# Attention and feed-forward in one kernel: the last third of a head group's scores as one stretch, five steps a group

## Chip, cores and metric

One core of one Trainium2 chip. The metric is the device time of one execution in microseconds (us). The kernel before took 3215.65 us in the median of three runs (3213.75 to 3222.26).

## What is computed

A transformer block over 16 batches of 512 rows and 512 columns: layernorm, attention with 32 heads of 16 columns (rotary positions, causal mask, softmax), a projection, layernorm and the residual, then a gated feed-forward of 512 to 1408 to 512, again with layernorms and a residual. Cut to what matters here:

```python
q, k, v = (split_heads(norm(x) @ W.T + b) for each of q, k, v)   # 32 heads of 16
scores  = einsum('bhqd,bhkd->bhqk', rope(q), rope(k)) / sqrt(16)
weights = softmax(where(causal, scores, -inf))
out     = einsum('bhqk,bhkd->bhqd', weights, v)
x = x + norm(out @ Wo.T + bo)
g, u = (norm(x) @ gate_w.T) * gate_s, (norm(x) @ up_w.T) * up_s
x = x + norm(((silu(g) * u) @ down_w.T) * down_s)
```

## The kernel before

**Groups.** Four heads are a group, eight groups a batch (`NG`), 128 groups in all. Each head lies in 32 partitions of its tiles, so its matmuls use 32 rows of TensorE, and four heads can be at work there side by side. Scores are made twice. "s" has queries in the partitions; VectorE masks it in place and takes each row's negated maximum (`maxima`, line 607; in the profile the rows `s<-s,mask` and `nm<-`). "st" has keys in the partitions, with the maximum already taken off by a third matmul (`mx`, `one`); ScalarE makes exp of it (`weights`, line 631, `pt<-st`), GpSimd masks the diagonal (`pt<-pt`). An "s" score needs two matmuls (high and low part of k: kh, kl), an "st" score three (kh, kl, mx).

**Thirds and steps.** The causal half of the 512 x 512 scores is cut into three thirds (lines 35 and 36): one block 512 wide; two blocks 128 and 384 wide; one block 256 wide. A group has `STEPS` = 6 steps, two for each third. Step i belongs to third i // 2 and pair i % 2 of the heads: `scores` (line 562) makes "st" for two heads of group n and "s" for the other two heads of a later group m, which is n + 1 in steps 0 and 1 and n + 2 from step 2 on. The lists of up to four heads are issued in rounds, one matmul of each head in turn; where the lists differ in length the last rounds have two matmuls. Such a run of score matmuls is called a stretch here.

**PSUM.** There are eight banks: one "st" tile of two banks (`ps_t`, line 87, a single buffer), two "s" tiles of one bank, one for the value products ("av"), three for dense work (`ps_d`). A stretch waits until the exp and the maxima of the one before it have left these tiles.

**Order.** Every instruction is issued through `InOrder` (line 39; its line 49 is the one that the profile names for all), which keeps the order of the program on each engine. `one_step` (line 792) fixes that order: first what was put off to this step (`later`), at step 0 the loads of q, kh and kl of group n + 2 (`load_group`), then the stretch of scores, at step 2 the transposition of the next group's maxima (`turn_maxima`, sent by DMA at step 3 and read at the next group's step 0), then a share of dense work, then at step 3 `values` of the first third and at step 0 those of the second and third of the group before.

**Dense work.** Everything else that TensorE does (q, k, v, projection, gate, up, down, transpositions) is written as a list with costs (`MM` = 1, `M1` = 0.27 for the cheaper format, `TR` = 0.15). `run_list` (line 696) deals it out to the steps in equal shares; `batches` (line 951) makes one list for a batch's 48 steps, and a first list for 56 steps, from two groups ahead of the first batch on. Loads and stores stand in the same lists and go to SyncE's one queue in that order. A group's output is stored at the step after `values`; `sums` and `sums_2` (lines 678 and 687) fetch the softmax sums from DRAM 2 and 3 steps after it.

Of the kernel before, what the change touches and what calls it, by code (L numbers as in the profile page):

```python
# [10 lines left out]
FP = mybir.dt.float32  # L11
FR = mybir.dt.float32r
AF = mybir.ActivationFunctionType
# [5 lines left out]
P = 128  # L19
T = 512  # L20
# [5 lines left out]
NC = C // P  # L26
NG = H // 4
WIDTH = H * W + 32 - W + 1
STEPS = 6
MM = 1.0  # L30
TR = 0.15
M1 = 0.27
# [2 lines left out]
S_SETS = [[(3, 0, 512)], [(0, 384, 128), (2, 0, 384)], [(1, 0, 256)]]  # L35
ST_SETS = [[(0, 0, 512)], [(3, 0, 128), (1, 128, 384)], [(2, 0, 256)]]
# [15 lines left out]


class Block:

# [503 lines left out]

    def scores(self, n, m, i):

        third, pair = divmod(i, 2)
        ps = pm = None
        todo = []
        if 0 <= n < self.B * NG:
            ps = self.ps_t.tile([P, 2, T], FP, tag="st", name="st")
            q, ks, mx = self.qs[n], self.ks[n], self.mxs[n]
            for j in range(2):  # L570
                h = 32 * (2 * pair + j)
                r, r2 = slice(h, h + 32), slice(h, h + 2)
                todo.append([])
                for kb, at, w in ST_SETS[third]:
                    out, x = ps[:, j, at : at + w], q[r, T - w : T]
                    todo[-1] += [
                        (out, ks[0][r, ts(kb, P)], x, True, False),
                        (out, ks[1][r, ts(kb, P)], x, False, False),
                        (out, self.one[r2, :], mx[r2, T - w : T], False, True),
                    ]  # L580
        if 0 <= m < self.B * NG:
            if n < 0 and i % 2:
                both = self.ps_t.tile([P, 2, T], FP, tag="st", name="st")
                pm = [both[:, j, :] for j in range(2)]
            else:
                pm = [self.ps_s.tile([P, T], FP, tag="s", name="s") for _ in range(2)]
            q, ks = self.qs[m], self.ks[m]
            for j in range(2):
                h = 32 * (2 * (1 - pair) + j)
                r = slice(h, h + 32)  # L590
                todo.append([])
                for qb, at, w in S_SETS[third]:
                    out, x = pm[j][:, at : at + w], q[r, ts(qb, P)]
                    todo[-1] += [(out, x, ks[0][r, 0:w], True, False), (out, x, ks[1][r, 0:w], False, True)]

        for k in range(max((len(t) for t in todo), default=0)):
            for t in todo:
                if k < len(t):
                    out, l, r, first, last = t[k]
                    self.pe.matmul(out, l, r, start=first, stop=last)  # L600
        if ps is not None:
            self.weights(n, third, pair, ps)
        if pm is not None:
            for j in range(2):
                self.maxima(m, third, 2 * (1 - pair) + j, pm[j])

    def maxima(self, m, third, j, s):
        if m not in self.nms:
# [19 lines left out]

        self.later(1, put)

    def weights(self, n, third, pair, ps):
        w = sum(w for _, _, w in ST_SETS[third])
        if third < 2 or pair == 0:
            pt = self.tile([P, 2, T], "pt", bufs=4)
            self.pts[n, third, pair] = pt
        if third == 2:
            if pair:
                pt = self.pts[n, 2, 1] = self.pts[n, 2, 0]
            pt = pt[:, pair, :].rearrange("p (j t) -> p j t", j=2)
        self.act.activation(pt[:, :, :w], ps[:, :, :w], AF.Exp, scale=0.25)  # L640
        if third == 1:
            d = pt[:, :, 0 : 2 * P]
            pat = [[0, 2], [0, 2], [1, P]]
        else:
            d = pt[:, :, 0:P]
            pat = [[0, 2], [1, P]]
        self.pool.affine_select(out=d, in_=d, compare_op=ALU.is_ge, fill=0.0, base=0, pattern=pat, channel_multiplier=-1)

    def values(self, n, third):
        b, g = divmod(n, NG)  # L650
        if third == 0:
            self.avs[n] = self.ps_av.tile([P, T], FP, tag="av", name="av")
        av = self.avs[n]
        for kb, at, w in ST_SETS[third]:
            for j in range(4):
                h = 4 * g + j
                pt = self.pts[n, third, j // 2]
                pt = pt[:, j // 2, T // 2 * (j % 2) :] if third == 2 else pt[:, j % 2, :]
                self.pe.matmul(
                    av[32 * j : 32 * j + 32, T - w : T],  # L660
                    self.v17[b % 2][:, kb, h * W : h * W + 32],
                    pt[:, at : at + w],
                    start=(kb == 0),
                    stop=(third == 2),
                )
        for pair in range(2):
            del self.pts[n, third, pair]
        if third == 2:
            del self.ks[n], self.qs[n], self.mxs[n]
            ot = self.tile([P, T], "ot", bufs=1)  # L670
            self.act.copy(ot, self.avs.pop(n))
            i = (b % 2) * NC + g // 2
            self.later(1, lambda: self.sp.dma_start(out=self.od[i][P * (g % 2) : P * (g % 2) + P, :], in_=ot))
            if g % 2:

                self.later(8 if b == self.B - 2 and g < NG - 1 else 2, self.sums, b, g // 2)

    def sums(self, b, c):
        i = (b % 2) * NC + c
# [13 lines left out]
        self.later(2, lambda: self.pool.tensor_tensor(self.ocs[b, c], self.ocs[b, c], rc, ALU.mult))  # L693


    def run_list(self, L, steps):

        L = self.laid(L)
        total = sum(c for c, _ in L)
        done, i = 0.0, 0  # L700
        for s in range(steps):
            goal = total * (s + 1) / steps
            while i < len(L) and (done + L[i][0] / 2 < goal or s == steps - 1):
                L[i][1]()
                done += L[i][0]
                i += 1
            yield
# [242 lines left out]

    def batches(self):
        B = self.B
        work = self.run_list(self.first_list(), 56)
        self.load_group(0)
        for n, i0 in ((-2, 2), (-1, 0)):
            for i in range(i0, STEPS):
                self.one_step(work, n, i)
        for b in range(B):
            if b:
                if b < B - 1:  # L960
                    L = self.dense(b)
                    L += self.gate_ups(b - 1, b + 2 if b + 2 < B else None, b + 2 == B)
                    if b < B - 2:
                        L += self.downs(b - 1, b + 2)
                else:
                    down = [self.downs(b - 2, None, tbs, True, True) for tbs in ((0, 1), (2, 3))]
                    L = down[0] + self.dense(b, down[1]) + self.gate_ups(b - 1, None, True)
                work = self.run_list(L, NG * STEPS)
            for g in range(NG):
                for i in range(STEPS):  # L970
                    self.one_step(work, b * NG + g, i)
        L = [(0, lambda half=half: self.load_w(B - 1, "o", half)) for half in range(2)]
        work = self.run_list(L + self.downs(B - 2, None, (0, 1), True, True), STEPS + 2)
        for i in range(STEPS + 2):
            self.one_step(work, B * NG + i // STEPS, i % STEPS)
        for _, f in self.laid(self.last_list()):
            f()
# [61 lines left out]
```

## Time and profile before

| what | value |
|---|---|
| median of the runs | 3215.65 us |
| the profiled execution | 3215.86 us, its span 3214.0 us |
| mean granted TensorE clock | 0.984 |
| exp of 2 x 512 columns (`pt<-st`) | 1.024 us, 512 times |
| exp of 2 x 256 columns | 0.596 us, 256 times |
| maximum over 512, 384, 256, 128 columns (`s<-s,mask`) | 0.714, 0.567, 0.447, 0.312 us |
| reading out a maximum (`nm<-`) | 0.141 us, 2048 times |
| mask on GpSimd, 256 columns | 0.450 us, 512 times |

How to read it: "st<-q,kh" is a matmul that writes tile st from tiles q and kh; "PE" is TensorE's matmuls, "PEld" its weight loads, "DVE" VectorE, "ACT" ScalarE, "POOL" GpSimd, "SPq" SyncE's DMA queue. Matmuls overlap, so one matmul's duration is longer than the distance to the next start. A dense matmul in full fp32 stands as two records.

In the steady part a step's stretch starts after these medians from the last one, steps 0 to 5: 5.03, 3.67, 3.83, 4.78, 3.29 and 3.28 us. From a stretch's first start to the next dense start it takes 0.89 us (512 wide), 1.06 us (128 and 384) and 0.55 us (256 wide, steps 4 and 5).

### The profile page before, as it was taken

The page shows a single profiled execution, that of the slowest core. Times are in us where ns is not written, and L with a number is a line of the kernel's source. Part 1 is how long each engine was busy: PE and PEld are TensorE (multiplying, and loading weights), DVE is VectorE, ACT ScalarE, POOL GpSimd, SP SyncE. Part 2 cuts the span into 40 slices and gives each one's busy share as a digit, 9 for nine tenths or more (in the row PEclk, how much of TensorE's full clock was granted, in tenths as well). Part 3 has the DMA queues.
Part 4 walks back from the last instruction along what each step waited for, and adds up shares of the span by engine and source line. Part 5 has one row for each costly group of instructions (what it writes and reads, how often), then busy time and mean ns, then how long its engine had stood idle before and what let it go on. Part 6 is the DMA issues. An engine that isn't in the chain of part 4 may idle for free.

```text
span 3214.0 us, 59287 instructions
## 1 busy us (share of the span) xinstructions
PE 3097.9 (96%) x21258; PEld 1743.3 (54%) x21258; DVE 1888.0 (59%) x5911; ACT 1542.7 (48%) x2243; POOL 1383.9 (43%) x1933
## 2 busy tenths in 40 slices
PE   6889999999999999999999999999999999999988
PEld 2334555646556464655646455464655646455556
DVE  5465656556565665656566565665656566565633
ACT  5354545454554544545454554544455454453432
POOL 4143445443544534345443544534345453443343
PEclk9899999999999999999999999999999999999999
DMA  6454534445353443525345352543535345343422
GB/s 251 166 166 152 189 101 163 139 149 172 108 190 106 160 164 123 195 93 177 127 152 173 127 185 96 168 147 123 195 101 183 122 147 172 123 156 105 131 97 71
DMA packets 227441, 471.41 MB, mean 147 GB/s; under 512 B 40976, under 2 KB 45072, under 8 KB 226704
## 3 DMA queue, kind: packets, MB, share of 16 engines
q1 hardware_dynamic: 226704, 466.47, 43.1%
q8 instruction: 170, 2.79, 0.4%
q10 hardware_dynamic: 432, 1.05, 0.1%
q14 instruction: 135, 1.11, 0.1%
HBM read 345.79 MB, written 125.30 MB: 147 GB/s over the span
## 4 chain that ended last, share of the span: by engine, by line
PE 83%; DVE 2%; DMA 2%; ACT 2%; POOL 1%; issue 1%; SPq 0%; ACTq 0%; DVEq 0%; POOLq 0%
PE st L49 16%; PE pu L49 11%; PE pg L49 10%; PE av L49 9%; PE pd L49 9%; PE po L49 7%; PE pq L49 6%; PE pv L49 5%; PE pk L49 5%; PE s L49 3%; DMA kl<-kd 2%; PE px L49 1%; ACT pt L49 1%; DVE s L49 1%; PE pm L49 1%
## 5 line engine op out<-in xcount | busy, mean ns | idle before, releaser
L49 DVE CUSTOM_DVE_ANT_0 s<-s,mask 128x512 f32<-128x512 f32 (+1 forms) x2034 | 974.9, 510 | 713.8 <-PE s L49 530.8
L49 ACT ACTIVATE pt<-st 128x1024 f32<-128x1024 f32 (+1 forms) x768 | 677.0, 882 | 755.9 <-PE st L49 746.9
L49 POOL TENSOR_SCALAR_AFFINE_SELECT pt<-pt 128x256 f32<-128x256 f32 (+1 forms) x768 | 393.8, 513 | 1202.3 <-ACT pt L49 1200.0
L49 PEld LDWEIGHTS st<-q,kh 32*128 32x128 f32 x2048 | 191.3, 183 | 463.3 <-issue 225.6
L49 PE MATMUL st<-q,kh 32*128 32x512 f32 (+3 forms) x2048 | 411.2, 398 | 22.3 <-ACT pt L49 20.9
L49 PE MATMUL s<-kh,q 32*128 32x512 f32 (+1 forms) x2034 | 411.6, 399 | 17.2 <-DVE nm L49 8.8
L49 PE MATMUL s<-kl,q 32*128 32x512 f32 (+1 forms) x2034 | 340.7, 321 | 11.2 <-DMA kl<-kd 11.2
L49 PE MATMUL av<-pt,v 128*32 128x512 f32 (+3 forms) x4096 | 336.0, 447 | 0.0
L49 PE MATMUL st<-q,kl 32*128 32x512 f32 (+3 forms) x2048 | 333.5, 322 | 0.0
L49 PE MATMUL st<-mx,one 2*128 2x512 f32 (+3 forms) x2048 | 333.0, 321 | 0.0
L49 POOL TENSOR_TENSOR hl<-ht,hh 128x512 fp32r<-128x512 f32 (+1 forms) x192 | 229.6, 1196 | 184.3 <-ACT hh L49 176.7
L49 PE MATMUL pd<-wd,hl 128*128 128x512 f32 x704 | 288.9, 410 | 9.2 <-POOL hl L49 9.2
L49 PE MATMUL pd<-wd,hh 128*128 128x512 f32 x704 | 290.9, 413 | 2.2 <-ACT hh L49 2.2
L49 DVE DVE_READ_ACCUMULATOR2_ANT nm<- 128x1 f32 x2048 | 288.8, 141 | 0.0
L49 PE MATMUL pg<-xntf,wf 128*128 128x512 f32 x704 | 287.4, 408 | 1.5 <-ACT xntf L49 1.5
L49 PE MATMUL pu<-xntfl,wf 128*128 128x512 f32 x704 | 284.3, 404 | 0.0
L49 PE MATMUL pu<-xntf,wf 128*128 128x512 f32 x704 | 283.9, 403 | 0.0
L49 PE MATMUL pg<-xntfl,wf 128*128 128x512 f32 x704 | 281.5, 400 | 0.6 <-DVE xntfl L49 0.6
L49 PE MATMUL po<-w,oc 128*128 128x512 f32 x512 | 244.6, 610 | 3.7 <-DMA w<-in_wo 3.7
L49 PE MATMUL pq<-xnta,w 128*128 128x512 f32 x480 | 237.6, 626 | 6.9 <-ACT xntf L49 6.3
L49 PE MATMUL pk<-xnta,w 128*128 128x512 f32 x480 | 238.3, 615 | 4.3 <-DVE ya L49 3.7
L49 POOL TENSOR_TENSOR yl<-ya,yh 128x512 fp32r<-128x512 f32 x128 | 163.3, 1276 | 169.4 <-ACT yh L49 169.4
(118 smaller groups left out, 5021.8 us busy)
## 6 DMA issues: line engine op xcount, KB each, us to landing
wf<-wgs SPq DMA_DIRECT2D x176, 512.0 KB
q<-qd SPq DMA_DIRECT2D x128, 256.0 KB
kh<-kd SPq DMA_DIRECT2D x128, 256.0 KB
kl<-kd SPq DMA_DIRECT2D x128, 256.0 KB
od<-ot SPq DMA_DIRECT2D x128, 256.0 KB
w<-in_wo SPq DMA_DIRECT2D x34, 512.0 KB
xr<-in_x SPq DMA_DIRECT2D x66, 256.0 KB
w<-in_wq SPq DMA_DIRECT2D x32, 512.0 KB
```

Of the source, the lines that this page charges most:

```text
L49: return self.tc.keep_in_program_order(f(*args, **kwargs))
```

## The change

The last third gets one step for all four heads: `STEPS` is 5. The four heads' lists are issued in rounds of four, each list first the three "st" matmuls of a head of group n, then the two "s" matmuls of the same head of group m. Both write the same bank: "s" its first 256 columns, "st" its last 256. Heads 0 and 1 use the two banks of the "st" tile, heads 2 and 3 the two "s" tiles. exp runs first for heads 0 and 1 in one instruction while the maxima of heads 2 and 3 are taken, then for heads 2 and 3 in one instruction each, then come the maxima of heads 0 and 1. The masks on GpSimd stay one for each pair.

`run_list` deals dense work to the five steps in the shares 0.7, 0.95, 1.1, 0.95 and 1.3 (of five). What is put off by a number of steps keeps that number, but for one that goes from 8 to 7. The matmuls of the first two thirds, and their order, are the same.

```diff
-STEPS = 6
+STEPS = 5
+SHARES = 0.7, 0.95, 1.1, 0.95, 1.3
...
     def scores(self, n, m, i):
         third, pair = divmod(i, 2)
...
+        st = lambda: self.ps_t.tile([P, 2, T], FP, tag="st", name="st")
+        one = lambda: self.ps_s.tile([P, T], FP, tag="s", name="s")
+        if third == 2:
+            both = st()
+            banks = [both[:, 0, :], both[:, 1, :], one(), one()]
+            for j in range(4):
+                todo.append([])
+                if isn:
+                    todo[-1] += self.for_weights(n, third, j, banks[j][:, T // 2 :])
+                if ism:
+                    todo[-1] += self.for_maxima(m, third, j, banks[j])
+            self.turns(todo)
+            for pair in range(2):
+                if isn:
+                    parts = [(0, 2, both[:, :, T // 2 :])] if pair == 0 else [
+                        (j, 1, banks[2 + j][:, T // 2 :].unsqueeze(1)) for j in range(2)
+                    ]
+                    self.weights(n, third, pair, parts)
+                if ism:
+                    for j in (2, 3) if pair == 0 else (0, 1):
+                        self.maxima(m, third, j, banks[j])
+            return
...
+    def for_weights(self, n, third, j, ps):
+        q, ks, mx = self.qs[n], self.ks[n], self.mxs[n]
+        r, r2 = slice(32 * j, 32 * j + 32), slice(32 * j, 32 * j + 2)
+        L = []
+        for kb, at, w in ST_SETS[third]:
+            out, x = ps[:, at : at + w], q[r, T - w : T]
+            L += [
+                (out, ks[0][r, ts(kb, P)], x, True, False),
+                (out, ks[1][r, ts(kb, P)], x, False, False),
+                (out, self.one[r2, :], mx[r2, T - w : T], False, True),
+            ]
+        return L
...
+    def turns(self, todo):
+        for k in range(max(len(t) for t in todo)):
             for t in todo:
                 if k < len(t):
                     out, l, r, first, last = t[k]
                     self.pe.matmul(out, l, r, start=first, stop=last)
...
-        self.act.activation(pt[:, :, :w], ps[:, :, :w], AF.Exp, scale=0.25)
+        for j, k, ps in parts:
+            self.act.activation(pt[:, j : j + k, :w], ps[:, :, :w], AF.Exp, scale=0.25)
...
-                self.later(8 if b == self.B - 2 and g < NG - 1 else 2, self.sums, b, g // 2)
+                self.later(7 if b == self.B - 2 and g < NG - 1 else 2, self.sums, b, g // 2)
...
-        total = sum(c for c, _ in L)
-        done, i = 0.0, 0
+        shares = [SHARES[(s + first) % STEPS] for s in range(steps)]
+        total = sum(c for c, _ in L) / sum(shares)
+        done, goal, i = 0.0, 0.0, 0
         for s in range(steps):
-            goal = total * (s + 1) / steps
+            goal += total * shares[s]
...
-        work = self.run_list(self.first_list(), 56)
+        work = self.run_list(self.first_list(), 3 + 8 * STEPS + 3, 2)
```

`for_maxima` makes a head's "s" list in the same way as before, as a function of its own.

More of the change, by code (lines that the diff above doesn't have):

```diff
@@ L566, in scores @@
         todo = []
-        if 0 <= n < self.B * NG:
-            ps = self.ps_t.tile([P, 2, T], FP, tag="st", name="st")
-            q, ks, mx = self.qs[n], self.ks[n], self.mxs[n]
-            for j in range(2):
[L571 to L580, printed above, removed]
@@ L581, in scores @@
-        if 0 <= m < self.B * NG:
+        isn, ism = 0 <= n < self.B * NG, 0 <= m < self.B * NG
+        if not isn and not ism:
+            return
[20 more added lines that the diff above has]
+                        self.maxima(m, third, j, banks[j])
+            return
@@ L582, in scores @@
+        if isn:
+            ps = st()
+            for j in range(2):
+                todo.append(self.for_weights(n, third, 2 * pair + j, ps[:, j, :]))
+        if ism:
             if n < 0 and i % 2:
-                both = self.ps_t.tile([P, 2, T], FP, tag="st", name="st")
+                both = st()
                 pm = [both[:, j, :] for j in range(2)]
             else:
-                pm = [self.ps_s.tile([P, T], FP, tag="s", name="s") for _ in range(2)]
-            q, ks = self.qs[m], self.ks[m]
+                pm = [one() for _ in range(2)]
@@ L588, in scores @@
             for j in range(2):
[L589 to L596, printed above, removed]
+                todo.append(self.for_maxima(m, third, 2 * (1 - pair) + j, pm[j]))
@@ new lines, in scores @@
+        self.turns(todo)
+        if isn:
+            self.weights(n, third, pair, [(0, 2, ps)])
+        if ism:
+            for j in range(2):
+                self.maxima(m, third, 2 * (1 - pair) + j, pm[j])
+    def for_weights(self, n, third, j, ps):
[10 more added lines that the diff above has]
+        return L
@@ L597, in scores, with for_maxima @@
+    def for_maxima(self, m, third, j, pm):
+        q, ks = self.qs[m], self.ks[m]
+        r = slice(32 * j, 32 * j + 32)
+        L = []
+        for qb, at, w in S_SETS[third]:
+            out, x = pm[:, at : at + w], q[r, ts(qb, P)]
+            L += [(out, x, ks[0][r, 0:w], True, False), (out, x, ks[1][r, 0:w], False, True)]
+        return L
+    def turns(self, todo):
+        for k in range(max(len(t) for t in todo)):
             for t in todo:
@@ L600, in scores @@
                     self.pe.matmul(out, l, r, start=first, stop=last)
[L601 to L605, printed above, removed]
     def maxima(self, m, third, j, s):
@@ L629, in turn_maxima, with weights @@
         self.later(1, put)
-    def weights(self, n, third, pair, ps):
+    def weights(self, n, third, pair, parts):
         w = sum(w for _, _, w in ST_SETS[third])
@@ L693, in sums_2, with run_list @@
         self.later(2, lambda: self.pool.tensor_tensor(self.ocs[b, c], self.ocs[b, c], rc, ALU.mult))
-    def run_list(self, L, steps):
+    def run_list(self, L, steps, first=0):
         L = self.laid(L)
-        total = sum(c for c, _ in L)
-        done, i = 0.0, 0
+        shares = [SHARES[(s + first) % STEPS] for s in range(steps)]
+        total = sum(c for c, _ in L) / sum(shares)
+        done, goal, i = 0.0, 0.0, 0
         for s in range(steps):
-            goal = total * (s + 1) / steps
+            goal += total * shares[s]
             while i < len(L) and (done + L[i][0] / 2 < goal or s == steps - 1):
```

## Prediction

> **What bounds the kernel.** I read the page's head first, then the busy time by stretches of the span, then TensorE's waits in the steady part, then the timeline of TensorE through one group.
>
> The page's head:
>
> ```profile
> span 3214.0 us, 59287 instructions
> ...
> PE 3097.9 (96%) x21258; PEld 1743.3 (54%) x21258; DVE 1888.0 (59%) x5911; ACT 1542.7 (48%) x2243; POOL 1383.9 (43%) x1933
> ```
>
> The stretches (us, then the busy us of PE, PEld, DVE, ACT, POOL, the granted clock, DMA share, GB/s), two of them:
>
> ```profile
> 108.00:290.00 182.00, 158.34 (x1168) 68.51 (x1168) 94.92 (x340) 80.72 (x113) 57.38 (x84) 0.87 0.48 161
> ...
> 1520.00:1930.00 410.00, 406.33 (x2865) 233.46 (x2864) 249.09 (x783) 201.30 (x294) 178.56 (x250) 1.00 0.46 154
> ```
>
> TensorE's waits from 290 to 2880 us:
>
> ```profile
> PE s L49 <- DMA kl<-kd: 11.2, 13, 2.5
> PE st L49 <- ACT pt L49: 7.9, 27, 0.4
> PE pm L49 <- DVE ya L49: 6.1, 13, 0.5
> PE s L49 <- DMA kh<-kd: 3.6, 5, 1.1
> PE s L49 <- DVE nm L49: 2.8, 14, 0.5
> ```
>
> From 290 us to the end of the main loop PE is busy 99% at full clock, and all its waits are some 33 us of 2590. So it is TensorE's own sequence that sets the time: only fewer or shorter slots on PE help, and other engines matter only once they make PE wait. Only the first batch (108 to 290 us) is different: PE at 87% and a lower clock.
>
> But busy is not dense. One score stretch of the last third, in TensorE's timeline (start us, us):
>
> ```profile
> 1525.40 0.39 PE L49 MATMUL pg<-xntf,wf 128*128 128x512 f32 x1
> 1525.63 0.39 PE L49 MATMUL pg<-xntfl,wf 128*128 128x512 f32 x1
> 1525.95 0.39 PE L49 MATMUL st<-q,kh 32*128 32x256 f32 x2
> 1525.96 0.38 PE L49 MATMUL s<-kh,q 32*128 32x256 f32 x2
> 1526.17 0.28 PE L49 MATMUL st<-q,kl 32*128 32x256 f32 x2
> 1526.18 0.28 PE L49 MATMUL s<-kl,q 32*128 32x256 f32 x2
> 1526.30 0.28 PE L49 MATMUL st<-mx,one 2*128 2x256 f32 x2
> 1526.51 0.50 PE L49 MATMUL pg<-xntf,wf 128*128 128x512 f32 x1
> 1526.84 0.39 PE L49 MATMUL pg<-xntfl,wf 128*128 128x512 f32 x1
> ```
>
> The reader is to look at starts, not durations. Dense matmuls start every 0.23 us. A round of scores (one matmul for each of up to four row groups, all starting within 0.01 us) follows the last by 0.13 us here, 0.12 in the median of all such stretches. But the first round is followed after 0.22, the last after 0.21, and the dense matmuls at both edges are late: 0.32 and 0.33 instead of 0.23. The third round holds two matmuls, not four, and costs the same.
>
> **The change, part by part.**
>
> *The stretch, on PE.* Today the last third costs two such stretches a group. Each costs, from the dense start ahead (1525.63) to the second dense start behind (1526.84), 1.21, less two dense intervals (0.46): 0.75 us; two are 1.50. The new stretch has the same twelve "st" and eight "s" matmuls in five full rounds (three st, two s for each head) instead of 2 x 3 rounds. Its starts: 0.22 for the first, 3 x 0.12, 0.21 for the last, and 0.10 + 0.10 lateness at the edges = 0.99 us. Saved: 0.51 us a group (one round, and one pair of edges). 128 groups: 65 us. The two groups ahead of the first batch (maxima alone) lose one stretch each: about 1 us together.
>
> Here a rule speaks against the change. The Trainium skill (TensorE: Matmul & The Clock Gate, Part 3) says that a weight load overlaps matmuls in flight only when the row group differs. In the new stretch each row group goes through five matmuls on end, and every round needs a weight load into a row group that is still at work. By the rule a round would be 256 columns (0.11 us by the rows) and then the load of 0.18 us (the row of LDWEIGHTS st<-q,kh): 0.29 us, the two added rounds 0.58 instead of 0.24, the gain 0.17 us a group, 22 us in all. The trace already has this case: the loads for the second round start 0.11 us after the first round's matmuls in the same row groups, and the second round lasts 0.12. The 128/384 stretches run such chains six deep with no larger gap. I take 0.12.
>
> *What the readers of the scores do.* Before, exp (ScalarE) reads the st banks and the maxima (VectorE) read the s banks at once: 1526.64 and 1526.53. Now a head's two kinds share a bank. The Trainium skill (PSUM — Partial Sum Buffer, Terms) says that two engines in the same bank and partitions at once is an error; if the framework keeps them apart, they must take turns, which no row of before shows. Bounds: with no turns, heads 0 and 1 come free when the slower of the two is done, about 1.1 us after the last round; with turns, VectorE takes heads 2 and 3 (0.87 us for two 256-wide maxima), ScalarE meanwhile heads 0 and 1 (start 0.38 us after the last round in the median, 0.60 long), then VectorE heads 0 and 1: 0.98 + 0.87, or about 2.0 us. I take turns. Who waits for it: the first stretch of the next group, which needs those banks. Its cover is the dense work of the last step: 1.3/5 of a group's. A group is 23.55 us (1505.45 to 1529.00); less score stretches 2 x (1.10 + 1.27 + 0.75) = 6.24 and the value products 1.43 + 1.00 it leaves 14.88 us dense, so 3.87 us. In the worst tenth exp starts 2.4 us late, behind other ScalarE work: 2.4 + 0.6 + 0.87 = 3.9, just at the cover. Cost 0 in the median; bounds 0 and 0.1 us a group (13 us). Queued behind these on VectorE are the dense tails; four maxima on end take about 1.8 us there, which the 128/384 steps have today (last one done 2.0 us after the stretch) without PE stalling behind them. Three PSUM buffers of 8 x 0.23 us each cover it: 0.
>
> *One more exp.* Heads 2 and 3 lie in separate tiles, so one exp of 512 columns becomes two of 256. From the rows (1.024 us for 1024, 0.596 for 512) one of 256 is about 0.38: +0.17 us a group, 22 us on ScalarE, which is 48% busy. Off the path: 0. GpSimd's masks are as many as before.
>
> *Five steps with unequal dense shares.* The dense total is the same. Per step PE then takes 4.61, 3.93, 4.54, 5.10, 4.86 us (before: 5.01, 3.58, 3.75, 4.75, 3.23, 3.23). Dense cover behind a stretch was 2.48 us in each step (plus values in two); now it is 2.08 (plus 1.43 of values), 2.83, 3.27, 2.83 (plus 1.00) and 3.87. The shortest, 2.48, grows to 2.83, so the 10.7 us of waits for exp and maxima can shrink a little; I count 0, bounds -8 and +10.
>
> *What moves with the steps on SyncE's queue.* q, kh and kl are fetched at step 0 and used at step 2: 8.59 us before, 8.54 after; the 14.8 us of waits for kh and kl stay. The transposed maxima go out at step 3 for the next group's step 0: 11.2 us before, 10.0 after, and the trace shows no PE wait on them. The outputs' store precedes the load of the sums by one step: 3.58, now 3.93. All 0, bounds -3 and +8 together.
>
> *First batch.* Ten per cent of its time is PE waiting (13.0 us for exp, 4.9 for maxima), because it has little dense work to cover anything. One step fewer saves latency, the longer chain of the last third gives it back: 0 beyond the 0.51 counted, bounds -10 and +8.
>
> **The sum.** The profiled execution took 3215.86 us (span 3214.0 and 1.9 around it), 0.2 above the median of the three runs. 3215.9 - 65 - 1 = 3149.9; I say **3150 us**.
>
> **The rivals.**
>
> *More than that* (8%): the waits of the first batch and those for exp and maxima shrink too, -15 to -20: about 3132. For it: the longer covers. Against: those waits are small.
>
> *Partly given back* (12%): either the rule on weight loads holds for chains of four full rounds (3215.9 - 22 = 3194), or dense tails arrive late behind four maxima and PE waits 0.25 us a group (32 us: 3182). Against both: rows above.
>
> *Slower* (6%): the turns in the shared banks. If exp stands behind a ScalarE cast that itself waits for TensorE (the page has "hh" casts waiting on "pd"), VectorE stands still with it, dense tails fill the three PSUM buffers, and the next group's first stretch waits. It decides from 0.51 us a group on, that is when the chain of 2.0 us in the median is 4.4 us in the mean. At 0.8 us a group: +102 - 65 = 3253. Against it: even the worst tenth only reaches 3.9.
>
> *No change* (2%): the stretch is not one in effect, because PE must wait inside it for a reader of the shared bank. All twenty matmuls are issued ahead of the readers, so nothing in the order asks for it: 3216.
>
> **How the numbers follow.** The likeliest case has 72%, its own range 3138 to 3165. A measurement of this kernel can tell about 0.3% (10 us) from no change. Faster by more: 72 + 8 + 12 = 92%; within: 2%; slower: 6%. The range 3132 to 3185 leaves out slower and no change (8%), the upper part of "partly" (3%) and the lower half of "more" (4%).
>
> **What would show it.** Right: in the timeline, one stretch of twenty 256-wide matmuls a group, rounds 0.12 us apart, 0.79 us from its first start to the next dense start; group period 23.0 instead of 23.55; PE still near 99% in the steady part. Wrong: rounds 0.2 us or more apart (the weight rule); a PE idle entry "st <- ACT pt" or "st <- DVE nm" that grows to tens of us, at the 512-wide stretch at a group's start (the turns); dense matmuls waiting on VectorE tails right after the long step; or a longer wait for kl, kh or mx.

## The result and the profile after

| | median of the runs | against before, ratio (95% interval) |
|---|---|---|
| before, measured again | 3217.5 us | |
| after | 3221.0 us | 1.0015 (1.0004 to 1.0026) |

Forecast was 3150 us. What was measured is 0.15% slower, some 4 us: no change by the prediction's bound of 0.3%. The profiled execution has a span of 3218.8 us, against 3214.0.

The page's head and one stretch of the span (columns as before) say that TensorE now has less to do and stands more, and that its granted clock is no longer 1.00 in the steady part:

```profile
PE 3048.4 (95%) x21258; PEld 1740.6 (54%) x21258; DVE 1897.0 (59%) x5911; ACT 1554.9 (48%) x2371; POOL 1377.1 (43%) x1933
```

```profile
1520.00:1930.00 410.00, 397.07 (x2827) 230.16 (x2825) 246.32 (x768) 199.94 (x306) 176.26 (x248) 0.98 0.45 150
```

The merged stretch in TensorE's timeline:

```profile
1526.68 0.38 PE L50 MATMUL st<-q,kh 32*128 32x256 f32 x2
1526.69 0.39 PE L50 MATMUL s<-q,kh 32*128 32x256 f32 x2
1526.91 0.28 PE L50 MATMUL st<-q,kl 32*128 32x256 f32 x2
1526.91 0.28 PE L50 MATMUL s<-q,kl 32*128 32x256 f32 x2
1527.03 0.28 PE L50 MATMUL st<-mx,one 2*128 2x256 f32 x2
1527.03 0.28 PE L50 MATMUL s<-mx,one 2*128 2x256 f32 x2
1527.14 0.28 PE L50 MATMUL st<-kh,q 32*128 32x256 f32 x2
1527.15 0.28 PE L50 MATMUL s<-kh,q 32*128 32x256 f32 x2
1527.27 0.27 PE L50 MATMUL st<-kl,q 32*128 32x256 f32 x2
1527.27 0.28 PE L50 MATMUL s<-kl,q 32*128 32x256 f32 x2
1527.48 0.50 PE L50 MATMUL pu<-xntfl,wf 128*128 128x512 f32 x1
```

(The tiles "st" and "s" are now only names of banks; each row of x2 is two heads.) Rounds start 0.12 us apart, and 0.80 us pass from the first to the next dense start; 0.79 was forecast. So the saving is there. TensorE's waits from 290 to 2880 us show what stands against it:

```profile
PE st L50 <- DMA mx<-nml: 49.6, 13, 4.6
PE pm L50 <- DVE ya L50: 19.2, 13, 1.5
PE s L50 <- DMA kl<-kd: 8.5, 14, 1.1
PE st L50 <- ACT pt L50: 5.0, 14, 0.4
PE s L50 <- DMA kh<-kd: 3.6, 6, 1.5
```

The first line is new: thirteen times, once a batch, TensorE waits about 4 us (3.4 to 4.6) for the transposed maxima (mx), for which it had not waited at all in this part before. It waits in a group's first stretch, the 512-wide one, not in the merged one. One of these stops in TensorE's timeline:

```profile
1477.27 0.39 PE L50 MATMUL st<-q,kl 32*128 32x512 f32 x2
1477.28 0.39 PE L50 MATMUL s<-kl,q 32*128 32x512 f32 x2
1482.03 0.79 PE L50 MATMUL st<-mx,one 2*128 2x512 f32 x2 [4.36 <-DMA mx<-nml]
1482.75 1.11 PE L50 MATMUL px<-ident,xn 128*128 128x128 f32 x4
1483.65 2.77 PE L50 MATMUL pk<-xnta,w 128*128 128x512 f32 x3
```

and the stretches of the span around it, where the number behind POOL's count is the granted clock:

```profile
1474.20:1481.10 6.90, 3.47 (x15) 1.25 (x13) 5.04 (x16) 4.72 (x8) 5.23 (x9) 1.00 0.24 74
1481.10:1487.90 6.80, 5.87 (x22) 2.83 (x26) 0.73 (x2) 2.38 (x3) 2.19 (x3) 0.50 0.65 240
1487.90:1494.80 6.90, 6.32 (x56) 2.98 (x48) 2.89 (x8) 3.57 (x5) 2.83 (x4) 1.00 0.11 40
```

The stop costs twice: 4.36 us of standing, and then a clock of one half until 1487.9, 5.9 us of it with work to do, which loses some 3 us more.

Why mx is late stands in SyncE's queue. Before, at the same place:

```profile
1473.10 0.45 SPq L49 DMA_DIRECT2D rd<-sum  x1
1476.81 0.59 SPq L49 DMA_DIRECT2D xr<-rd  x1
1477.49 0.58 SPq L49 DMA_DIRECT2D mx<-nmh  x1
1478.13 0.56 SPq L49 DMA_DIRECT2D mx<-nml  x1
1481.46 0.33 SPq L49 DMA_DIRECT2D xr<-in_x  x1
```

and after:

```profile
1470.99 0.33 SPq L50 DMA_DIRECT2D xr<-in_x  x1
1471.43 0.38 SPq L50 DMA_DIRECT2D rd<-sum  x1
1477.11 0.58 SPq L50 DMA_DIRECT2D xr<-rd  x1
1477.80 0.58 SPq L50 DMA_DIRECT2D mx<-nmh  x1
1478.42 0.57 SPq L50 DMA_DIRECT2D mx<-nml  x1
```

mx stands behind xr<-rd, the load of the reciprocal softmax sums, which shares two buffers (xr) with the loads of x for the projection's residual. Before, the last of those x loads comes behind mx (1481.46). After, it comes ahead of the sums (1470.99), so the load of the reciprocals needs the buffer of the x block before it, which GpSimd frees in this line of its timeline, at 1477.08:

```profile
1475.81 1.27 POOL L50 TENSOR_TENSOR x<-x,xr 128x512 f32<-128x512 f32 x1 [0.26 <-ACT x L50]
```

The reciprocals (rd) had landed at 1473.75 by the records of their semaphore, so 3.3 us of the delay are the buffer alone. The transposition (pm) and the stretch that needs mx stand so in TensorE's timeline, before:

```profile
1467.46 0.28 PE L49 MATMUL pm<-ident,nm 128*16 128x128 f32 x1
...
1481.29 0.50 PE L49 MATMUL st<-q,kh 32*128 32x512 f32 x2
...
1481.86 0.40 PE L49 MATMUL st<-mx,one 2*128 2x512 f32 x2
```

and after (the stretch at 1476.93, its mx at 1482.03):

```profile
1463.64 0.28 PE L50 MATMUL pm<-ident,nm 128*16 128x128 f32 x1
...
1476.93 0.49 PE L50 MATMUL st<-q,kh 32*128 32x512 f32 x2
```

From pm to the issue of the second half of mx it is 14.8 us, before 10.7. The stretch that needs it comes 13.3 us after pm, before 13.8. By the records of its semaphore, that half landed 3.5 us after its issue, just ahead of TensorE's use at 3.6; before it landed after 2.6 us and was used after 3.7 (1478.13 to 1481.86). So before had about 1 us to spare here, and between 0.7 and 1.4 us from landing to use in the thirteen such places from 290 to 2700 us. A later issue by 4.1, a stretch earlier by 0.5 and a transfer longer by 0.9, less that 1.0, make 4.5 us, beside 4.36 of idle time in the row. Why the transfer took longer is not shown.

### The profile page after: what moved, and what is told of

The parts are those of the page before. It is cut to its first block, busy times and chain, and to the rows that moved or that the text cites. A ratio compares the mean times of both kernels' runs of the same rounds, so it can differ in the third digit from the quotient of the medians.

```text
span 3218.8 us, 59518 instructions
## 1 busy us (share of the span) xinstructions
PE 3048.4 (95%) x21258; PEld 1740.6 (54%) x21258; DVE 1897.0 (59%) x5911; ACT 1554.9 (48%) x2371; POOL 1377.1 (43%) x1933
## 4 chain that ended last, share of the span: by engine, by line
PE 76%; DVE 6%; POOL 4%; DMA 4%; ACT 3%; issue 2%; SPq 1%; POOLq 0%; ACTq 0%; DVEq 0%
PE st L50 14%; PE pu L50 11%; PE pg L50 10%; PE pd L50 9%; PE av L50 8%; PE pq L50 6%; PE pv L50 5%; PE pk L50 4%; PE po L50 4%; PE s L50 2%; DVE ln_st L50 2%; DMA kl<-kd 2%; DMA mx<-nml 1%; PE px L50 1%; POOL ln_rstd L50 1%
## 5 line engine op out<-in xcount | busy, mean ns | idle before, releaser
L50 DVE CUSTOM_DVE_ANT_0 s<-s,mask 128x512 f32<-128x512 f32 (+1 forms) x1782 | 873.1, 520 | 692.8 <-PE s L50 645.7
L50 ACT ACTIVATE pt<-st 128x1024 f32<-128x1024 f32 (+1 forms) x640 | 601.4, 940 | 791.0 <-PE st L50 577.8
L50 POOL TENSOR_SCALAR_AFFINE_SELECT pt<-pt 128x256 f32<-128x256 f32 (+1 forms) x768 | 378.0, 495 | 1156.8 <-ACT pt L50 1147.2
L50 PE MATMUL st<-q,kh 32*128 32x512 f32 (+3 forms) x1792 | 361.0, 399 | 21.2 <-DVE nm L50 10.2
L50 PEld LDWEIGHTS st<-q,kh 32*128 32x128 f32 x1792 | 167.1, 183 | 387.0 <-issue 217.6
L50 PE MATMUL st<-mx,one 2*128 2x512 f32 (+3 forms) x1792 | 301.4, 331 | 49.8 <-DMA mx<-nml 49.6
L50 PE MATMUL s<-kh,q 32*128 32x512 f32 (+1 forms) x1782 | 339.5, 384 | 8.8 <-DMA kh<-kd 6.0
L50 PE MATMUL s<-kl,q 32*128 32x512 f32 (+1 forms) x1782 | 298.5, 325 | 8.9 <-DMA kl<-kd 8.9
L50 PE MATMUL st<-q,kl 32*128 32x512 f32 (+3 forms) x1792 | 296.0, 326 | 0.0
L50 PE MATMUL pk<-xnta,w 128*128 128x512 f32 x480 | 250.8, 652 | 3.7 <-DVE ya L50 3.3
```

Of the source, the lines that this page charges most:

```text
L50: return self.tc.keep_in_program_order(f(*args, **kwargs))
```

## The experiments

**mx first.** The changed kernel, with mx ahead of everything else that is put off to step 3:

```diff
-        self.later(1, put)
+        self.todo[self.step + 1].insert(0, (put, ()))
```

> The changed kernel; only the two small DMAs of the transposed maxima (mx) are put at the head of what is put off to step 3, ahead of the sums' DMAs on SyncE's queue. Theory (the gain of the merged stretch is there, and is eaten once a batch by mx standing behind the load of the reciprocal sums on that queue, plus the lower clock after each such stop): the 13 waits of 3.5 to 4.6 us vanish, the clock is back at 0.98 or more, and the time is 3148 to 3165 us. Rival (dense tails and shared banks eat the gain, mx only marks where PE would have waited anyway): the waits move to other names and the time stays within 3205 to 3225 us.

Measured: 3138.5 us, 0.974 of before (0.9721 to 0.9759). No wait on mx is left among TensorE's waits. One edit on SyncE's queue gives 82 us back (3221.0 less 3138.5), and the 49.6 us of standing are gone.

**The kernel before, mx first.** The same edit there.

> The kernel before with the same one edit (mx at the head of step 3). Theory: before had hardly a wait on mx (4 us in all), so 3210 to 3220 us, no change that can be measured; the edit is worth something only together with the five steps. Rival (the order of SyncE's queue is worth some 60 us by itself): 3150 to 3180 us.

Measured: 3220.9 us, 1.0005 (0.9996 to 1.0015). The order of the queue is worth nothing by itself: before, mx was late in the queue too, but landed in time.

**The sums a step later.** The changed kernel, mx in its old place, what stands ahead of it moved away:

```diff
-                self.later(7 if b == self.B - 2 and g < NG - 1 else 2, self.sums, b, g // 2)
+                self.later(7 if b == self.B - 2 and g < NG - 1 else 3, self.sums, b, g // 2)
```

> The changed kernel; mx keeps its place, but the fetch of the softmax sums is put off by one step more (3 instead of 2), so that the load of their reciprocals comes to SyncE's queue a step behind mx. Theory (mx was late only for what stood ahead of it on that queue): the waits on mx fall to a few us and the time to 3135 to 3165 us, as with mx put first. Rival (mx itself, its place at the head, or its transfer, is what matters): the waits stay and the time is 3205 to 3225 us.

Measured: 3143.0 us, 0.9768 (0.975 to 0.9786), and no wait on mx from 290 to 2880 us. The second way to the same gain, which does not touch mx: it was late for what stood ahead of it.

**The kernel before, mx late.** `self.later(2, put)` in place of `self.later(1, put)`, nothing else.

> The kernel before with the mx DMAs put off by one step more (step 4 instead of 3), nothing else. Theory (before had once a batch only about 1 us to spare between the arrival of mx and its use, hidden because nothing waited yet): a wait on mx of 2 to 4 us once a batch, 30 to 55 us in all, and the clock falls with it: 3240 to 3275 us. Rival (mx has much to spare, three steps or 11 us less some 3 us): 3210 to 3222 us.

Measured: 3276.0 us, 1.0173 (1.0155 to 1.0191), with this line at the head of TensorE's waits:

```profile
PE st L49 <- DMA mx<-nml: 32.1, 13, 3.4
```

So the loss appears in the kernel before as well, without a merged stretch, and 32 us of standing cost 58 us of time: 1.8 for one. (For the change it is 82 over 49.6, 1.7.) It also measures the room that before had: mx went out some 4.4 us later (15.0 us after pm instead of 10.6), landed 1.8 instead of 2.6 us after its issue, and the wait was 2.5 us, which again leaves about 1 us.

**The merged stretch in six steps.** The merged stretch at step 4, no scores in step 5, equal shares:

```diff
-STEPS = 5
-SHARES = 0.7, 0.95, 1.1, 0.95, 1.3
+STEPS = 6
+SHARES = (1.0,) * 6
...
+        if i == 5:
+            return
```

(with 8 instead of 7 for the late sums, and 56 steps for the first list, as before.)

> The merged stretch alone: six steps with equal shares of dense work, all four heads of the last third in step 4, and no scores in step 5 (dense work alone). mx keeps its three steps. Theory: the merged stretch is worth 0.51 us a group, so 3145 to 3165 us, with few waits on mx. Rival (the shared banks or the four maxima on end cost what the stretch saves): 3205 to 3225 us.

Measured: 3190.2 us, 0.9909 (0.9891 to 0.9928): between the two. No wait on mx, and 1.2 us on the maxima, so neither the queue nor the shared banks took the rest. The waits that are longer than before are others:

```profile
PE pm L50 <- DVE ya L50: 23.0, 13, 2.3
PE px L50 <- ACT xn L50: 11.7, 14, 0.9
```

They are 29 us more than before had on these (6.1 on pm). Mx first, though, has 18.8 us on pm as well. Between 260 and 2900 us the clock was at one half ten times, nine of them right behind a wait of pm (with mx first six times, one of them behind pm). The waits come once a batch, where a transposition happens to stand right behind VectorE's or ScalarE's part of a dense block; that this is a matter of how the lists fall is argued, not shown.

**Equal shares.** The changed kernel with 1.0 for each of the five steps.

> The changed kernel with equal shares of dense work in the five steps. It moves the projection's loads of x against the sums on SyncE's queue. Theory (the stop is an accident of which load stands ahead of the sums): the stop once a batch changes in length or goes; 3140 to 3225 us, and the time follows the waits on mx at some 1.7 us for each us waited. Rival (five steps leave mx too little time whatever stands ahead of it): the same 50 us of waits, 3210 to 3230 us.

Measured: 3251.6 us, 1.0099 (1.0081 to 1.0118). Neither expectation held. 37.1 us of waits on mx stayed, and two new ones came, 28.8 on the maxima and 21.0 on xn. So this run could not tell the two apart; the next one splits it.

**Equal shares, mx first.**

> mx first, and equal shares. The dense work behind the merged stretch falls from 3.9 to 3.0 us; exp and the maxima take turns there and are done 2.1 us after its last round. Theory (the turns are covered either way): within 10 us of the kernel with mx first, 3130 to 3150 us. Rival (the unequal shares are what keeps the turns in the shared banks covered): over 3160 us, with PE waits on exp or maxima at the 512-wide stretch.

Measured: 3183.1 us, 0.9893 (0.9873 to 0.9913). The rival was right: the unequal shares are worth 45 us. TensorE's waits:

```profile
PE st L50 <- DVE nm L50: 29.0, 27, 1.3
PE px L50 <- ACT xn L50: 21.0, 13, 1.6
```

The first is the merged step's four maxima. One place (exp of heads 0 and 1, a dense tail and the first maximum on VectorE, the last maximum, the group's first stretch):

```profile
481.67 0.60 ACT L50 ACTIVATE pt<-st 128x512 f32<-128x512 f32 x1
481.73 0.75 DVE L50 SCALAR_TENSOR_TENSOR ya<-pq,cols,turn 128x512 f32<-128x512 f32 x1 [2.15 <-POOL yl L50]
482.40 0.42 DVE L50 CUSTOM_DVE_ANT_0 s<-s,mask 128x256 f32<-128x256 f32 x1
484.02 0.14 DVE L50 DVE_READ_ACCUMULATOR2_ANT nm<- 128x1 f32 x1
484.31 0.49 PE L50 MATMUL st<-q,kh 32*128 32x512 f32 x2 [0.92 <-DVE nm L50]
```

The merged stretch's last round starts at 480.33. VectorE comes to the first maximum only 2.1 us later, behind a dense tail (ya) that had itself waited for GpSimd, and then takes four on end until 484.16: 3.8 us after that round, with about 3.0 us of dense work to cover them. Exp of heads 0 and 1 had ended before the first maximum began, so it is VectorE's lateness and the four maxima in one step that cost here, not the taking of turns with ScalarE.

**A long last step alone.** mx first, shares 0.925 four times and 1.3.

> mx first; shares 0.925 in the first four steps and 1.3 in the last. Equal shares with mx first took 3183 us, with 29 us of PE waits on the maxima at the first stretch of a group and 21 us on xn; the shares of the change took 3138. Theory (the dense work behind the merged stretch is what covers the turns in the shared banks): the waits on the maxima at the 512-wide stretch fall below 5 us, and the time to 3138 to 3160 us. Rival (the lists merely fall differently against the steps, whatever stands behind the merged stretch): 3165 to 3190 us, and the waits on the maxima stay over 20 us.

Measured: 3144.8 us, 0.9773 (0.975 to 0.9797). The waits on the maxima are 0.6 us, those on xn are gone:

```profile
PE s L50 <- DVE nm L50: 0.6, 1, 0.6
```

So of the shares it is the 1.3 behind the merged stretch that counts. How it does so is not split: there is more dense work behind the stretch, but the four maxima also end sooner, 3.0 us after its last round at most, where with equal shares and mx first it was 4.3, because other dense tails stand ahead of them on VectorE. How the rest is dealt to the first four steps makes no difference that these runs show (3134.9 to 3150.4 us here, 3134.2 to 3146.1 with the shares of the change).

**The transposition behind the dense work.** mx first, and step 2's `turn_maxima` called after that step's dense share.

> mx first, and the transposition of the maxima (pm) issued behind step 2's dense work instead of ahead of it. pm waited 19 us for VectorE's ya, 13 times, since it stood right behind the stretch. Theory: those waits go, mx goes out 3 us later but is still in time: 3115 to 3138 us. Rival (pm then waits for another dense tail, or mx is late again): 3138 to 3200 us.

Measured: 3210.7 us, 0.9978 (0.9967 to 0.9989); a miss, and slower than the rival too. The wait moved on and grew: 26.8 us of "PE pk <- DVE ya" and 7.4 of "PE pd <- DVE nml", and the clock stood at one half fifteen times between 260 and 2900 us (six times with mx first). By the ledger below, standing and clock are some 2.7 us a batch of the 4.4 that it lost against mx first; the rest is not explained. The best version stays the one with mx first.

**The batch as a ledger.** From the trace: a steady batch of eight groups (mean of 14, from one transposition of maxima to the one eight groups on), the gaps between TensorE's matmul records in it, and half of the time at half clock. The last column is the first less the other two; it is rough, since the last two overlap where the clock is low while PE stands.

| kernel | batch us | PE idle | lost to the clock | rest |
|---|---|---|---|---|
| before | 190.15 | 2.40 | 0.24 | 187.5 |
| after | 192.24 | 6.28 | 3.05 | 182.9 |
| mx first | 186.59 | 3.02 | 0.61 | 183.0 |
| sums a step later | 185.97 | 2.90 | 0.00 | 183.1 |
| mx first, equal shares | 189.47 | 4.64 | 0.85 | 184.0 |
| merged, six steps | 189.15 | 4.02 | 1.22 | 183.9 |
| before, mx late | 194.01 | 4.79 | 1.58 | 187.6 |
| transposition behind | 190.96 | 4.10 | 2.19 | 184.7 |

The rest falls from 187.5 to 183.0 with the merged stretch and five steps, 4.5 us a batch or 0.56 a group; 0.51 was forecast. After alone gives back more than all of it: 3.9 us of standing and 2.8 of clock. In its 14 steady batches it lost 29 us against before; the whole came out level because the first batch took 14 us less, and the start and the end 10 us less.

## Why the prediction was wrong, point by point

*The stretch on PE: right.* 0.80 us for the 0.79 of the sum, 0.12 between rounds; the rule that a weight load overlaps only another row group's matmuls did not hold here. The load for the third round starts with the second round's matmuls (1526.91), in the same row groups, and the third round's matmuls follow at 1527.03:

```profile
1526.91 0.19 PEld L50 LDWEIGHTS st<-mx,one 2*128 2x128 f32 x2
```

*Readers taking turns: right in the median, not in the tail.* In the trace after, the last round of the stretch starts at 1527.27, VectorE and ScalarE start together on different heads, and VectorE is done with heads 0 and 1 at 1529.40, 2.1 us after that round (2.0 forecast):

```profile
1527.62 0.43 DVE L50 CUSTOM_DVE_ANT_0 s<-s,mask 128x256 f32<-128x256 f32 x1 [1.54 <-PE s L50]
1527.64 0.60 ACT L50 ACTIVATE pt<-st 128x512 f32<-128x512 f32 x1 [2.29 <-PE s L50]
...
1528.35 0.47 DVE L50 CUSTOM_DVE_ANT_0 st<-st,mask 128x256 f32<-128x256 f32 x1
...
1528.91 0.43 DVE L50 CUSTOM_DVE_ANT_0 st<-st,mask 128x256 f32<-128x256 f32 x1
...
1529.26 0.14 DVE L50 DVE_READ_ACCUMULATOR2_ANT nm<- 128x1 f32 x1
```

These are four maxima on end; no turn made VectorE wait here. The chain of 3.9 us in the worst tenth, "just at the cover", did not come: in after it is 2.8 us there, and 3.0 at most. With equal shares and mx first it reached 4.3 us, against 3.0 of cover, and cost 29 us of standing, but by VectorE's lateness, where the prediction had ScalarE's. The waits for exp and maxima fell from 10.7 to 5.2 us, within the bounds.

*SyncE's queue: the step that failed.* The prediction had the maxima go out at step 3 for the next step 0, "11.2 us before, 10.0 after, and the trace shows no PE wait on them", bounds -3 and +8 with the rest of the queue. It took the program's place for the time of issue. In the trace of before mx was issued 10.5 to 11.1 us after pm in that place of thirteen batches, and so only 3.3 to 3.9 us ahead of its use, not 11.2; a missing wait was read as room to spare where there was about 1 us. The measured term is 49.6 us of standing and 82 us of time. That a longer wait for mx would show the sum wrong, the prediction did say. It counted the same queue's other loads by their steps alone, too; that the dealing of dense work moves the x loads against the sums, past which mx must come, it did not look at.

*The clock: missing.* No term stood for what a stop costs after it is over. Each us of standing cost 1.7 to 1.8 us of time. By the ledger the half clock makes 0.56 (before, mx late, against before) to 0.75 us (after against mx first) for each us of standing, so it is most of that excess; the remainder is not explained.

*Dense tails: partly.* The wait of pm for ya rose from 6.1 to 19.2 us, and no term of the sum named it; it is there with mx first as well (18.8), which still reaches the gain.

*First batch: the gain was larger than counted.* From the second to the tenth transposition of maxima it took 150.9 us before, 136.5 after, 139.0 with mx first: -12 to -14, where eight times 0.51 is 4. The bound of -10 beyond that just held it. With it, mx first is 3138.5 us, below the 3150 of the sum.

*The rivals.* None had this cause. "No change" had 2%, for a merged stretch that waits inside for a reader of its bank; the stretch that does wait inside is another, a group's first, and for the DMA of mx. That the time came out at the old one is chance: a gain and a loss of about the same size.

What stays open: why equal shares and six steps leave about 1 us a batch more in the last column of the ledger than the unequal ones.

## What to carry to other kernels

A transfer that nobody waits for may still have little room: measure from its issue to its landing to its first use, in the tightest place and not in the median, before counting a shorter window at nothing. When work is dealt out anew, write down for the in-order DMA queue what will stand ahead of each small urgent transfer, and which buffer each of those waits for; here the urgent one belonged at the head. And a single stop of TensorE can be dearer than its length, here 1.7 to 1.8 us for each us.

## What the runs showed of the hardware

After a stop TensorE's granted clock often stood at 0.50 for one or two stretches of 3.4 us. In the kernel after, each of the thirteen stops on mx (3.4 to 4.6 us) brought it, and eleven of the fourteen stretches at half clock between 260 and 2900 us last 6.8 us. With stops of 2.5 us in the mean (before, mx late), seven of the ten last 3.4 us. The Trainium skill (TensorE: Matmul & The Clock Gate, Part 1) tells of the half clock after idle windows of 3.4 us; in these runs shorter stops also brought it, though not each time: eleven of the thirteen stops of 2.1 us with the transposition behind the dense work, and six of the thirteen of 1.6 us with mx first and equal shares.
